# A four-layer graph network on one core: another order of the turns in the first stage, SAGE's weights multiplied while the lists are closed, and neighbour lists transposed by TensorE

## The chip, the cores and the metric

The kernel runs on one core of one Trainium2 chip. The metric is the time of one execution on the device in microseconds (us), lower is better; the given time is the median of three runs. Beside these there is one profiled execution, from which all durations of single instructions are taken.

A core has five engines that run their own queues in order and wait for each other through semaphores: TensorE (PE, matrix products), VectorE (DVE), ScalarE (ACT), GpSimd (POOL) and SyncE (SP). Here SyncE issues the ordinary transfers, GpSimd the gathers of single rows.

## The reference

Input are x (3327 x 512) and an adjacency matrix adj (3327 x 3327, 0 or 1). Four layers follow, each with a residual: `h = relu(layernorm(x)); x = x + layer(h, adj)`. Layers 0, 2 and 3 are graph attention with 8 heads of 64 columns, layer 1 is SAGE. Cut to what is computed:

```
# attention (layers 0, 2, 3), per head
Wh = h @ W
e  = leaky_relu(s_dst[i] + s_src[j], 0.2); e = where(adj > 0, e, -9e15)
out = softmax(e, over j) @ Wh        # layer 0: batch norm and relu; layers 2, 3: elu
# SAGE (layer 1)
agg = mask @ h / max(deg, 1)
out = relu(concat(h @ W_self + b_self, agg @ W_nb + b_nb) @ W_comb + b_comb)
```

In SAGE there is nothing between the two products, so W_self and W_nb can be multiplied by their halves of W_comb once, ahead of the data.

## The kernel before

The 3327 nodes are padded to 26 blocks of 128 rows (NB = 26). The adjacency is sparse and uneven, and the kernel lists for each of 52 groups of 64 rows which columns have any edge to the group. A fixed table, PLAN, says how many chunks of 128 columns a group takes whole ("dense") and how many chunks of listed columns. Attention then fetches rows of a table in DRAM, the dense ones by SyncE (line 1310), the listed ones by GpSimd's indirect gathers with the list idx as row numbers (line 1315).

The stages stand one after another:

1. **The turns** (`lists`, the loop over c at the end of the with block, and class `Projection`). Turn c handles three things. *Compare*: block c + 1 of adj is loaded as int32 (adj_i, line 1108, three buffers) and compared to 0 into a bf16 mask (adj_b, two buffers). Two blocks of three take a plain compare (line 1111) and are counted by ScalarE (`count`, line 1119); the third takes a compare with a sum (line 1113). `alone` (line 1122) sets one column from the count. *Words* (`gathered`): 26 small products of the mask with wsel pack 16 mask bits to a word (words_ps, line 1129); ScalarE copies the words out (line 1130), and VectorE derives from the same products which columns are absent from a group (none, line 1136). *Projection of layer 0* in a pipeline over turns: `first()` scales the products of block c - 3 into v_row (line 696), splits r_full into r_half and r_rest (lines 798 and 799), and transposes block c - 1 (h_ps, line 706); `second()` transposes r_half (tr_ps, line 724), and multiplies block c - 2 by the small and the large weight (sd_ps, line 739; wh_ps, line 742). SyncE writes table and r_dram (lines 699 and 729). After turns 3 and 6 `Products.layer` prepares small weights of other layers.
2. **Closing** (`closing`): VectorE adds up past (line 1145), TensorE makes 26 pairs of small products (shift_ps, lines 1149 and 1152), and then twelve passes over 3327 columns move each column number to its place in the list (lines 1164 to 1176); lines 1179 and 1180 leave the lists in shift, one group per partition: in partitions 0 to 63 the columns with exactly one edge to the group, in 64 to 127 those with several, which fill the group's chunks from the other end. Three last turns of the projection are interleaved with the first passes.
3. **Lists through DRAM**: SyncE and GpSimd write shift to DRAM (lines 1219, eight transfers each), read it back with one list chunk per row (line 1226), TensorE mirrors and adds the two halves by products with permutations (lines 1236 to 1241), and VectorE makes idx (lines 1246 to 1248). A fits test (lines 1251 to 1274) sets ok, on which a branch chooses the sparse path.
4. **Attention of layer 0** (`attend`): for each unit, VectorE makes the weights (mx, wgt, vw; lines 1544 to 1558) and TensorE accumulates facc (lines 1578 and 1589). Beside it runs a generator, `beside`: one step per unit, first SAGE's 8 weight products and 2 bias products of four 128x512 matrix products each (lines 1656 to 1681), then the sums for the batch norm (bsum_ps).
5. Batch norm, SAGE, and the attention of layers 2 and 3, which the change leaves alone.

In the stages 1, 2 and 4 the order on TensorE, VectorE and ScalarE is the order of the program, written out by hand (`manual_schedule`); SyncE's and GpSimd's queues, and all queues outside those blocks, are ordered by the compiler's scheduler. The loop that matters:

```
for c in range(NB):
    proj.first()
    alone(c)
    compare(c + 1)
    gathered(c)
    proj.second()
    count(c + 1)
```

## Time and profile before

| | |
|---|---|
| median of three runs | 2641.61 us (2631.7 to 2646.2) |
| profiled execution, its own time | 2360.66 us |
| its span | 2358.9 us |
| mean granted TensorE clock | 0.868 |
| TensorE busy | 1853.9 us (79%) |
| VectorE busy | 1703.4 us (72%) |
| ScalarE busy | 1102.6 us (47%) |
| GpSimd busy | 1167.0 us (49%) |
| DMA | 562.66 MB, mean 239 GB/s |

The page divides the span by engine, then by line; views of the trace give a stretch of time, the instructions in order of time, and the waits. In a row of the timeline stand the start (us), the duration (us), engine, line and operation, the tiles written and read, the shape, and in brackets how long the engine had been idle and what ended that. A row of stretches gives its length and then busy time and number of instructions for TensorE's products, its weight loads, VectorE, ScalarE and GpSimd, then the granted clock (1 is full), the DMA engines' share and GB/s. A row of waits gives the sum in us, how often, and the longest.

### The profile page before, as it was taken

Reading aid. Unit: us, or ns where it says so; the run is one execution under the profiler, and the core shown is the slowest. Engines: PE = TensorE matmul, PEld = TensorE weight load, DVE = VectorE, ACT = ScalarE, POOL = GpSimd, SP = SyncE. Lnnn points to the kernel's source line nnn. Section 1 sums busy time; section 2 is a strip of 40 time slices with the busy share of each in tenths; the row PEclk is TensorE's granted clock in tenths of the full one; section 3 lists DMA queues with packets and bytes.
Section 4 is the critical chain, followed back from the end, with each engine's and each line's share of the span. In section 5 each row is a group of like instructions: output and inputs, shape, how many; then the busy total and the mean of one; then the engine's idle time right before and its main releaser. Section 6 shows DMA issues by size and latency. Waiting matters only on the chain. (4 is left out here: it accounts for less than half of the span.)

```text
span 2358.9 us, 42783 instructions
## 1 busy us (share of the span) xinstructions
PE 1853.9 (79%) x14795; PEld 1033.1 (44%) x14795; DVE 1703.4 (72%) x3061; ACT 1102.6 (47%) x4123; POOL 1167.0 (49%) x1227
## 2 busy tenths in 40 slices
PE   5888316897888769899999947889888857777875
PEld 4555204454545424233333325555454435544443
DVE  5555966888889984044555559888777749999996
ACT  3566102355666644133333203678887812444543
POOL 1000023566777500477777536655655236776772
PEclk8788657999999979999999967889889867788787
DMA  7776118897889655688888698787777458888883
GB/s 278 261 286 234 32 68 294 272 326 261 266 257 296 216 187 205 217 252 258 265 257 264 207 280 273 238 254 241 226 242 240 137 209 251 272 281 261 278 284 116
DMA packets 205951, 562.66 MB, mean 239 GB/s; under 512 B 37359, under 2 KB 43597, under 8 KB 202399
## 3 DMA queue, kind: packets, MB, share of 16 engines
q0 software_dynamic: 93504, 328.25, 45.0%
q1 hardware_dynamic: 112222, 231.59, 28.3%
q8 instruction: 120, 1.97, 0.3%
q14 instruction: 105, 0.85, 0.1%
HBM read 496.47 MB, written 63.25 MB: 237 GB/s over the span
## 5 line engine op out<-in xcount | busy, mean ns | idle before, releaser
L1315 POOL DMA_INDIRECT rows_e<-table,idx x654 | 627.3, 959 | 358.2 <-issue 151.5
L1578 PE MATMUL facc<-vw,ones_of 128*64 128x260 f32 x2616 | 445.2, 455 | 73.6 <-DVE vw L1544 58.4
L1589 PE MATMUL facc<-rows_s,wgt 128*64 128x65 f32 x7200 | 349.1, 249 | 166.5 <-DVE wgt L1558 112.4
L1589 PEld LDWEIGHTS facc<-rows_s,wgt 128*64 128x64 f32 x7200 | 294.9, 159 | 286.6 <-DVE wgt L1558 140.6
L1544 DVE TENSOR_TENSOR vw<-rows_e,w_of 128x1040 f32<-128x1040 f32 (+1 forms) x270 | 395.7, 1466 | 9.5
L1315 POOL DMA_INDIRECT z_rows<-z_dram,idx x291 | 279.7, 961 | 228.9 <-PE sage_acc L1867 154.1
L1315 POOL DMA_INDIRECT rows_s<-table,idx x219 | 212.7, 971 | 228.9 <-PE facc L1589 147.4
L1558 DVE TENSOR_TENSOR wgt<-mx,mask 128x1024 f32<-128x1024 f32 (+1 forms) x255 | 280.3, 1099 | 42.4 <-ACT mask L1456 26.0
L1554 DVE TENSOR_TENSOR mx<-r_bc,rows_s 128x1024 f32<-128x1024 f32 (+1 forms) x255 | 280.6, 1101 | 40.5 <-DMA rows_s<-table 28.6
L1405 ACT ACTIVATE fhp<-sums,rd 64x64 f32<-64x64 f32 x816 | 215.6, 334 | 185.2 <-DVE rd L1398 177.3
L1578 PEld LDWEIGHTS facc<-vw,ones_of 128*64 128x64 f32 x2616 | 196.5, 156 | 219.9 <-issue 91.4
L1867 PE MATMUL sage_acc<-z_rows,z_mask 128*64 128x512 f32 x622 | 165.4, 604 | 13.0 <-DMA z_rows<-z_dram,idx 12.8
L1219 POOL DMA_DIRECT2D list_b<-shift x8 | 4.1, 515 | 316.5 <-DVE shift L1180 316.5
L1818 DVE TENSOR_TENSOR s_o<-n_ps,sage_b 128x512 f32<-128x512 f32 x26 | 18.0, 692 | 167.0 <-PE n_ps L1815 163.3
L1850 ACT CAST z_mask<-mask 128x128 f32<-128x128 uint8 (+1 forms) x201 | 51.3, 287 | 162.2 <-PE sage_acc L1867 159.9
L742 PE MATMUL wh_ps<-fWt,hT 128*128 128x512 f32 x208 | 121.3, 737 | 0.0
L1392 ACT COPY sums<-facc 128x260 f32<-128x260 f32 x153 | 56.3, 368 | 136.4 <-PE facc L1578 135.2
L1405 ACT ACTIVATE bn_y<-sums,rd 64x64 f32<-64x64 f32 x408 | 107.7, 334 | 2.9 <-DVE rd L1398 1.3
L1496 DVE TENSOR_REDUCE w_of<-r_of 128x16 f32<-128x48 f32 (+1 forms) x270 | 61.4, 227 | 62.1 <-PE r_of L1488 37.0
L1815 PE MATMUL n_ps<-fWx,bn_y 128*128 128x512 f32 x208 | 97.3, 610 | 0.0
L1352 PE MATMUL r_bc<-r_two,fones 2*128 2x512 f32 x156 | 85.3, 547 | 14.4 <-DMA r_two<-r_dram 8.8
L924 PE MATMUL p_wh<-fWt,hT 128*128 128x512 f32 x208 | 96.0, 605 | 0.3 <-ACT hT L919 0.3
(260 smaller groups left out, 2888.5 us busy)
## 6 DMA issues: line engine op xcount, KB each, us to landing
adj_i<-in_adj SPq DMA_DIRECT2D x26, 1664.0 KB
rows_s<-table SPq DMA_DIRECT2D x46, 528.0 KB
table<-v_row SPq DMA_DIRECT2D x78, 264.0 KB
rows_s<-table SPq DMA_DIRECT2D x62, 264.0 KB
rows_s<-table SPq DMA_DIRECT2D x23, 632.0 KB
fin_x<-fx SPq DMA_DIRECT2D x52, 256.0 KB
rows_e<-table,idx POOLq DMA_INDIRECT x654
rows_s<-table SPq DMA_DIRECT2D x31, 316.0 KB
```

The source lines that it names most:

```text
L742: nc.tensor.matmul(wh, hT[:, kc, :], self.Wt[:, kc, :], start=(kc == 0), stop=(kc == KC - 1))
L924: nc.tensor.matmul(wh, hT[:, kc, :], self.Wt[:, kc, :], start=(kc == 0), stop=(kc == KC - 1))
L1315: nc.gpsimd.indirect_dma_start(out=dst, out_offset=None, in_=src[:, :], in_offset=bass.IndirectOffsetOnAxis(ap=idx[:, k : k + 1], axis=0))
L1352: nc.tensor.matmul(rb, ones[0:2, :].bitcast(F32R), rrs.pop(j).bitcast(F32R), start=True, stop=True)
L1405: nc.scalar.mul(hp[o0 : o0 + GB, h * F : (h + 1) * F], sm[mine, q, 0:F], rd[mine, q, :])
L1544: nc.vector.tensor_tensor(vw[:, :n], gt[:, :n, : H * (F + 1)].rearrange("p k (h x) -> p k h x", x=F + 1), w[:, :n].unsqueeze(3).to_broadca ...
L1554: nc.vector.tensor_tensor(mx[:, :n], rbs[j].unsqueeze(1).to_broadcast(full), T.unsqueeze(3).to_broadcast(full), ALU.max)
L1558: nc.vector.tensor_tensor(wt[:, :n], mx[:, :n], mk.unsqueeze(2).to_broadcast(full), ALU.mult)
L1578: nc.tensor.matmul(accs[g][v * GB : (v + 1) * GB, :sw].rearrange("p (q x) -> p q x", x=F + 1), ones_of[i][:, k, :], by[:, v], start=f, stop=l,
L1589: nc.tensor.matmul(accs[g][v * GB : (v + 1) * GB, q * (F + 1) : (q + 1) * (F + 1)], wt[:, k, h, :], gt[:, k, h * (F + 1) : (h + 1) * (F + 1)],
L1815: nc.tensor.matmul(ps, y[:, b, kc * P : (kc + 1) * P], Wx[:, 0, kc, :], start=(kc == 0), stop=(kc == KC - 1))
L1867: nc.tensor.matmul(acc[u * GB : (u + 1) * GB, :], m, z, start=f, stop=l)
```

## The change

- *Turns*: `compare(c + 1)` moves to the head of the turn, and `second()` ahead of `gathered(c)`. The buffers stay three and two.
- *SAGE's weights*: the weight and bias products leave `beside` and become a generator `merged()`, stepped six times after each of the later passes of the closing and to its end behind them. They use the buffers of adj_i and the words' PSUM ring; their results still go to wx_dram, from where attention of layer 0 loads them (`w2`) as its generator's first act.
- *Fits*: the test becomes `fits()`, called between the sixth and the seventh pass of the closing; the counts' reciprocals go with it.
- *Lists*: no DRAM. TensorE transposes the 64 x 128 pieces of shift, mirrors the upper half by products with rev, and adds both in PSUM. A list's columns are now at k * 64 + g, so idx grows from 291 to 640 columns, and the gathers' column numbers follow.

```diff
-        self.first, self.n, self.at, self.nm = [], 0, [], 0
-        for g, (dense, mixed, pure) in enumerate(PLAN):
-            self.first.append(self.n)
-            self.n += mixed + pure
+        self.at, self.nm, self.most = [], 0, max(m + p for _, m, p in PLAN)
+        for dense, mixed, pure in PLAN:
             self.at.append(self.nm)
             self.nm += dense + mixed + pure
...
         dense, mixed, pure = PLAN[g]
-        f = self.first[g]
-        src = [(True, c) for c in range(dense)] + [(False, f + pure + k) for k in range(mixed)]
-        src += [(False, f + k) for k in range(pure)]
+        src = [(True, c) for c in range(dense)] + [(False, (pure + k) * HALF + g) for k in range(mixed)]
+        src += [(False, k * HALF + g) for k in range(pure)]
         return [(self.at[g] + i, d, k) for i, (d, k) in enumerate(src)]
...
+        capr = lp.tile([1, 2, G], F32, name="cap_row")
+        for g, (_, mixed, pure) in enumerate(PLAN):
+            for k, n in enumerate((mixed + pure, mixed)):
+                if g == 0 or PLAN[g][1:] != PLAN[g - 1][1:]:
+                    e = next((j for j in range(g, G) if PLAN[j][1:] != PLAN[g][1:]), G)
+                    nc.vector.memset(capr[:, k, g:e], float((2 - k) * NP - n * P))
+        nc.sync.dma_start(bias, t["L1_gnn_b_comb"].partition_broadcast(P))
...
+            def fits():
+
+                hp_ = lps.tile([1, 2, HALF], F32, name="none_ps", tag="words_ps")
+                nc.tensor.matmul(
+                    hp_.rearrange("p c g -> p (c g)"),
+                    ones_bf[:, 0:1],
+                    past[:, NB, :, :].rearrange("p c g -> p (c g)"),
+                    start=True,
+                    stop=True,
+                )
+                hr = lp.tile([1, 2, HALF], F32, name="none_row")
+                nc.vector.tensor_copy(hr, hp_)
+                nc.vector.tensor_tensor(hr[:, 0, :G], hr[:, 0, :G], hr[:, 1, :G], ALU.add)
+                nc.vector.tensor_tensor(capr, capr, hr[:, :, :G], ALU.subtract)
+                over = lp.tile([1, 1], F32, name="over")
+                nc.vector.tensor_reduce(over, capr.rearrange("p k g -> p (k g)"), AX.X, ALU.max)
+                fit = lp.tile([1, 1], I32, name="fit")
+                nc.vector.tensor_scalar(fit, over, 0.0, None, ALU.is_le)
+                nc.vector.tensor_tensor(prods.ok, prods.ok, fit, ALU.mult)
+                nc.vector.tensor_scalar_max(rdeg, rdeg, 1.0)
+                nc.vector.reciprocal(rdeg, rdeg)
+
+            def merged():
+
+                def held():
+                    w = ap.tile([P, NP], I32, name="adj_i", tag="adj_i", bufs=3)
+                    return w.bitcast(F32)
+
+                spot = held()[:, : 6 * D].rearrange("p (k o) -> p k o", o=D)
+                cols, Wcs = [], []
+                for k, bn in enumerate(("L1_bs", "L1_bn")):
+                    Wc = held()[:, : KC * D].rearrange("p (k o) -> p k o", o=D)
+                    nc.sync.dma_start(Wc, t["L1_gnn_W_comb"][k * D : (k + 1) * D, :].rearrange("(kc p) o -> p kc o", p=P))
+                    bcol = lp.tile([P, KC, 1], F32, name=f"b_col{k}")
+                    nc.sync.dma_start(bcol[:, :, 0], t[bn])
+                    cols.append(bcol)
+                    Wcs.append(Wc)
+                yield
+                ps = None
+                for k, wn in enumerate(("L1_WsT", "L1_WnT")):
+                    Wc = Wcs[k]
+                    for fc in range(KC):
+                        nc.sync.dma_start(spot[:, 2 + fc % 2, :], t[wn][fc, :, :, :].rearrange("p k o -> p (k o)"))
+                        if fc == 0:
+                            yield
+                            b_bc = spot[:, k, :].rearrange("p (k o) -> p k o", o=P)
+                            nc.scalar.copy(b_bc, cols[k].to_broadcast([P, KC, P]))
+                            ps = lps.tile([P, D], F32, name="fb_ps", tag="words_ps")
+                            for kc in range(KC):
+                                nc.tensor.matmul(ps, b_bc[:, kc, :], Wc[:, kc, :], start=(kc == 0), stop=(kc == KC - 1))
+                                yield
+                            nc.vector.tensor_tensor(bias, bias, ps, ALU.add)
+                        else:
+                            yield
+                        WT = spot[:, 2 + fc % 2, :].rearrange("p (k o) -> p k o", o=P)
+                        ps = lps.tile([P, D], F32, name="fwx_ps", tag="words_ps")
+                        for kc in range(KC):
+                            nc.tensor.matmul(ps, WT[:, kc, :], Wc[:, kc, :], start=(kc == 0), stop=(kc == KC - 1))
+                            yield
+                        nc.scalar.copy(spot[:, 4 + fc % 2, :], ps)
+                        nc.sync.dma_start(wx_dram[k, fc, :, :], spot[:, 4 + fc % 2, :])
+
             prods.layer(0, lps, "words_ps")
             compare(0)
             count(0)
             proj.begin()
             for c in range(NB):
+                compare(c + 1)
                 proj.first()
                 alone(c)
-                compare(c + 1)
+                proj.second()
                 gathered(c)
-                proj.second()
                 count(c + 1)
                 if c in (3, 6):
                     prods.layer(c // 3, lps, "words_ps")
@@ -1198,84 +1247,58 @@
                 table[:, ROW:].rearrange("(c p) w -> p c w", p=P),
                 words.rearrange("p c b w -> p c (b w)").bitcast(I32),
             )
-            close = closing()
+            close, make = closing(), merged()
             next(close)
+            next(make)
             while proj.left():
                 proj.first()
                 next(close, None)
                 proj.second()
                 next(close, None)
+            fits()
             for _ in close:
+                for _ in range(6):
+                    next(make, None)
+            for _ in make:
                 pass
 
...
-        zero = lp.tile([P, P], F32, name="zero")
-        nc.gpsimd.memset(zero, 0.0)
-        ra = lp.tile([P, NT, P], F32, name="rows_a")
-        rb = lp.tile([P, NT, P], F32, name="rows_b")
-        for i, (dst, p0, rows_) in enumerate(((la, 0, ra), (lb, HALF, rb))):
-            eng = (nc.sync, nc.gpsimd)[i]
-            for g0, ng, cap in ls.runs:
-                f = ls.first[g0]
-                eng.dma_start(
-                    dst[f : f + ng * cap, :].rearrange("(g k) e -> g (k e)", k=cap),
-                    shift[p0 + g0 : p0 + g0 + ng, : cap * P],
-                )
-            if NT * P > NCH:
-                eng.dma_start(dst[NCH:, :], zero[: NT * P - NCH, :])
-            for q in range(NT):
-                eng.dma_start(rows_[:, q, :], dst[q * P : (q + 1) * P, :])
         with tc.tile_pool(name="lset2_ps", bufs=1, space=PSUM) as lps:
-            slots = lp.tile([P, NT * P], F32, name="slots")
-            per = lp.tile([P, NT, NT * P], F32, name="perm")
-            for q in range(NT):
-                nc.vector.tensor_scalar(per[:, q, :], mir, float(q * P), None, ALU.is_equal)
-            tb = lp.tile([P, NT * P], F32, name="tb")
-            assert NT * P <= BANK
-            pa = lps.tile([P, BANK], F32, name="pa", tag="pa")
-            for q in range(NT):
-                nc.tensor.matmul(pa[:, : NT * P], rb[:, q, :], per[:, q, :], start=(q == 0), stop=(q == NT - 1))
-            nc.vector.tensor_copy(tb, pa[:, : NT * P])
-            pb = lps.tile([P, BANK], F32, name="pb", tag="pb")
-            nc.tensor.matmul(pb[:, : NT * P], rev, tb, start=True, stop=False)
-            for q in range(NT):
-                nc.tensor.matmul(pb[:, q * P : (q + 1) * P], ra[:, q, :], ident, start=False, stop=(q == NT - 1))
-            nc.vector.tensor_copy(slots, pb[:, : NT * P])
-
-            s = slots[:, :NCH]
-            nv = lp.tile([P, NCH], F32, name="nv")
-            nc.vector.tensor_scalar(nv, s, 0.0, float(NP), ALU.is_equal, ALU.mult)
-            nc.vector.tensor_tensor(nv, nv, s, ALU.add)
-            nc.vector.tensor_scalar(idx, nv, -1.0, float(NP - 1), ALU.add, ALU.min)
...
+            per = BANK // HALF
+            lo, hi = slice(0, HALF), slice(HALF, 2 * HALF)
+            tb = lp.tile([P, J, HALF], F32, name="tb")
+            for r0 in range(0, J, per):
+                n = min(per, J - r0)
+                pb = proj.psum.tile([P, per, HALF], F32, name="pb", tag="wh_ps", bufs=2)
+                for r in range(r0, r0 + n):
+                    j = J - 1 - r
+                    nc.tensor.matmul(
+                        pb[:, r - r0, :], shift[hi, j * P : (j + 1) * P], ident[hi, hi], start=(r == r0), stop=(r == r0 + n - 1)
+                    )
+                (nc.scalar.copy if r0 else nc.vector.tensor_copy)(tb[:, r0 : r0 + n, :], pb[:, :n, :])
+            s = lps.tile([P, -(-J // per) * per, HALF], F32, name="slots", tag="slots")
+            for r0 in range(0, J, per):
+                n = min(per, J - r0)
+                for k in range(r0, r0 + n):
+                    nc.tensor.matmul(s[:, k, :], shift[lo, k * P : (k + 1) * P], ident[lo, lo], start=(k == r0), stop=False)
+                last = [(g0, ng, cap) for g0, ng, cap in ls.runs if cap > r0]
+                for i, (g0, ng, cap) in enumerate(last):
+                    m = min(cap, r0 + n) - r0
+                    nc.tensor.matmul(
+                        s[:, r0 : r0 + m, g0 : g0 + ng],
+                        rev,
+                        tb[:, J - cap + r0 : J - cap + r0 + m, g0 : g0 + ng],
+                        start=False,
+                        stop=(i == len(last) - 1),
+                    )
+            nv = lp.tile([P, J, HALF], F32, name="nv")
+            nc.vector.tensor_scalar(nv, s[:, :J, :], 0.0, float(NP), ALU.is_equal, ALU.mult)
+            nc.vector.scalar_tensor_tensor(
+                idx.rearrange("p (k g) -> p k g", g=HALF), nv, -1.0, s[:, :J, :], ALU.add, ALU.add
             )
...
-            nc.sync.dma_start(bias, t["L1_gnn_b_comb"].partition_broadcast(P))
...
-                Wc = work[:, : KC * D].rearrange("p (k o) -> p k o", o=D)
-                nc.sync.dma_start(Wc, t["L1_gnn_W_comb"][k * D : (k + 1) * D, :].rearrange("(kc p) o -> p kc o", p=P))
-                bcol = wp.tile([P, KC, 1], F32, name="b_col", tag="b_col", bufs=1)
-                nc.sync.dma_start(bcol[:, :, 0], t[bn])
...
-                nc.vector.tensor_tensor(bias, bias, ps, ALU.add)
-                for fc in range(KC):
-                    WT = spot[1 + fc % 2].rearrange("p (k o) -> p k o", o=P)
-                    nc.sync.dma_start(WT, t[wn][fc, :, :, :])
-                    yield
-                    ps = wps.tile([P, D], F32, name="fwx_ps", tag="beside", bufs=1)
-                    for kc in range(KC):
-                        nc.tensor.matmul(ps, WT[:, kc, :], Wc[:, kc, :], start=(kc == 0), stop=(kc == KC - 1))
-                        yield
-                    nc.scalar.copy(spot[3], ps)
-                    nc.sync.dma_start(wx_dram[k, fc, :, :], spot[3])
...
-        idx = kp.tile([P, ls.n], I32, name="idx")
+        idx = kp.tile([P, ls.most * HALF], I32, name="idx")
         rdeg = kp.tile([P, NP // P], F32, name="rdeg")
+        bias = kp.tile([P, D], F32, name="sage_b")
+        wx_dram = ldram.tile([2, KC, P, D], F32, name="wx_dram")
```

## The prediction

> **What bounds the kernel now.** Outside the profiled span lie only 2360.66 - 2358.9 = 1.8 us, so sums are made in the span. The three timed runs have a median of 2641.6 us, 281 us more than the profiled execution; nothing in the profile says where these lie. I carry my difference over in microseconds; in proportion it would be 1.12 times as large.
>
> I read the busy shares of the page first, then the busy time by stretches: the change touches only the first 520 us.
>
> ```profile
> PE 1853.9 (79%) x14795; PEld 1033.1 (44%) x14795; DVE 1703.4 (72%) x3061; ACT 1102.6 (47%) x4123; POOL 1167.0 (49%) x1227
> ...
> 200.00:250.00 50.00, 46.46 (x311) 27.47 (x310) 32.64 (x93) 29.40 (x111) 0.00 (x0) 0.84 0.54 177
> 250.00:270.00 20.00, 6.63 (x16) 3.50 (x15) 17.35 (x19) 1.99 (x10) 0.00 (x0) 0.59 0.04 14
> 270.00:290.00 20.00, 4.40 (x8) 1.48 (x6) 19.69 (x16) 0.45 (x2) 0.00 (x0) 0.67 0.04 14
> 290.00:310.00 20.00, 0.00 (x0) 0.00 (x0) 19.55 (x14) 0.00 (x0) 0.00 (x0) 0.50 0.00 0
> ```
>
> No engine bounds the whole. Up to about 233 us the turns run (projection, compares, words); 245 to 325 us is VectorE alone, closing the lists, with TensorE and the DMAs (share 0.04) free; then the lists go through DRAM, and attention of layer 0 begins at 343 us. These stages are serial, so a microsecond in one is a microsecond of the end.
>
> Next, the waits inside the turns, and from the timeline a turn at full clock, the start of another, and one with a stall:
>
> ```profile
> DVE v_row L696 <- PE wh_ps L742: 30.0, 14, 4.8
> PE words_ps L1129 <- DVE adj_b L1122: 27.1, 15, 4.4
> DVE adj_b L1111 <- DMA adj_i<-in_adj: 19.6, 10, 3.8
> ```
>
> ```profile
> 226.60 0.27 PE L724 MATMUL tr_ps<-fident,r_half 128*16 128x128 f32 x1
> 227.52 3.68 PE L742 MATMUL wh_ps<-fWt,hT 128*128 128x512 f32 x8
> 231.03 0.60 PE L706 MATMUL h_ps<-fident,ln_x 128*128 128x128 f32 x4
> 231.47 0.91 PE L1129 MATMUL words_ps<-wsel,adj_b 128*128 128x10 bf16 x26
> ```
>
> ```profile
> 129.86 0.19 PE L1129 MATMUL words_ps<-wsel,adj_b 128*128 128x10 bf16 x1 [2.30 <-DVE adj_b L1122]
> 129.90 0.37 PE L724 MATMUL tr_ps<-fident,r_half 128*16 128x128 f32 x1
> 130.07 3.62 DVE L1113 TENSOR_SCALAR_CACHE_REDUCE adj_b<-adj_i 128x3328 bf16<-128x3328 int32 x1 [0.26 <-DMA adj_i<-in_adj]
> 131.64 5.79 PE L742 MATMUL wh_ps<-fWt,hT 128*128 128x512 f32 x8
> ...
> 138.29 1.88 DVE L1111 TENSOR_SCALAR adj_b<-adj_i 128x3328 bf16<-128x3328 int32 x1
> ```
>
> The reader is to see that a turn costs TensorE 5.6 us (226.60 to 232.24 between two transposes tr_ps) if nothing stalls, that the long compare (3.6 us) lies under the wh_ps products, and that after a stall of 2.30 us the same products take 5.79 instead of 3.68 us.
>
> **The turns.** In the changed program's queues VectorE's order becomes: none of block c, compare of c+2, v_row, r_half; TensorE's: h_ps, tr_ps, sd_ps, wh_ps, then words of block c. none waits for ScalarE's copy of the words, and tr_ps waits for r_half. So the end of one turn's words releases copy, none, compare, v_row, r_half, and only then the next tr_ps: the compare, hidden before, stands in TensorE's path. What waits behind it is v_row and r_half on VectorE, all products behind tr_ps on TensorE, and on SyncE the table's write.
>
> The gap, by starts in the trace: ScalarE's copy 0.35 (L1130) with 0.09 of hand-over; none 0.23 (140.09 to 140.32); compare 1.80 (138.29 to 140.09) or 3.54 (130.07 to 133.61); v_row 0.60 (137.47 to 138.07); r_half and hand-over 0.22. Sum 3.29, or 5.03 us in every third turn. The transposes h_ps (0.60) fall inside it. TensorE from tr_ps to the words' end: 0.92 + 3.51 + 0.91 = 5.34 us. So 8.63 or 10.37 us a turn at full clock.
>
> The clock: the stall of TensorE before the last words' product and the length of the wh_ps behind it, over the stage: 1.38, 1.99, 2.30, 2.57, 3.43 and 4.39 us gave 5.06, 5.98, 5.79, 5.36, 5.04 and 6.42 us; of six stalls under 1 us two gave over 5 us, four 3.68. From tr_ps to the end of wh_ps these six took 7.71, 7.53, 6.28, 6.29, 6.77 and 7.96, mean 7.09 against 4.60: 2.5 us lost. [...] By the rows, where 1.38 us was enough six times in six, all 22 turns lose 2.5 us: 55 us. I take the rows.
>
> From tr_ps of turn 3 to the last words' end, before: 39.76 to 232.38 = 192.6 us. After: turn 3 itself 5.34, 14 short turns of 8.63, 7 long of 10.37, turn 25 without compare 1.49 + 5.34: 205.6; the clock 55; the two weight layers (32 small matmuls, 7.0 us at L507, run in a gap that is there anyway) 4 each, between 0 and 10: 268.6. **+76 us** (at full clock +21). DMA waits (20 + 4 us) vanish: adjacency loads are issued in the middle of turn k-3 for the compare in k-1, some 1.4 turns or 15 us, and landed in 7 us (141.49 to 148.56). ScalarE's count (3.0 + 0.2 us) moves behind the words' copy, ends 3.6 us after the words, when VectorE comes to its reader; hidden, and beyond that it delays only words, 5 us later. Turns 0 to 2 end about 2.5 us later (each compare precedes the products, and the fourth block's is long); after the last turn wh_ps no longer stands before the lists' products (-1.8: VectorE's 1.0 us wait at L1157, 0.8 of order).
>
> **SAGE's weights.** Moved: 40 products of 128x512 f32 (0.86 us each warm, two at 0.43 as in wh_ps), ten ScalarE copies of 0.6 us, two bias adds of 0.69, and SyncE's loads and stores of 6.3 MB. In the closing VectorE alone is the path: it gains the two adds and the fits (eight operations, 1.74 us): **+3.1**. Free of charge otherwise if TensorE is done when shift is ready. Its transposes stand behind all forty products in its queue. The first 4 run by 285 us; 36 start when none_row is copied, near 290.4 us of the old time: 36 x 0.86 + 2 for a cold start, and a last group that waits for the second bias add (323.3 + 3.5): 327 us, against shift at 325.5 + 3.1 = 328.6. Covered by 1.6 us only; cold they end at 290.4 + 36 x 1.72 = 352, 24 us late.
>
> What attention of layer 0 loses of work:
>
> ```profile
> 367.69 0.62 ACT L1666 COPY fmake<-b_col 128x512 f32<-128x512 f32 x1 [11.31 <-DMA b_col<-in_L_bs]
> 368.55 1.22 DVE L1558 TENSOR_TENSOR wgt<-mx,mask 128x1024 f32<-128x1024 f32 x1 [7.03 <-ACT mask L1456]
> ```
>
> ScalarE stood at the copy of b_col, the mask behind it, VectorE 7.0 us for the mask. From 360 to 515 us (the last copy of the weights) VectorE was busy 123.6 us, 0.80; from 550 to 800 us 220.8 us, 0.88. At that rate 123.6 us take 140: -15. By bytes: 6.3 MB at the 290 GB/s of that stretch, -22. Against it, the 2 MB load of fWx moves from 519 us to the attention's first loads and lies ahead of rows on SyncE: up to 7 us. I take **-17**, between -7 (the stall alone) and -28.
>
> **The lists.** From shift's end to idx and the gathers:
>
> ```profile
> 324.00 1.49 DVE L1180 SCALAR_TENSOR_TENSOR shift<-at,shift 128x1280 f32<-128x1280 uint16 x1
> 325.52 2.47 SPq L1219 DMA_DIRECT2D list_a<-shift  x8
> 332.94 4.21 PE L1236 MATMUL pa<-perm,rows_b 128*128 128x384 f32 x6 [56.00 <-DMA rows_b<-list_b]
> 340.97 0.29 DVE L1248 TENSOR_SCALAR idx<-nv 128x291 int32<-128x291 f32 x1
> 343.82 1.04 POOL L1315 DMA_INDIRECT rows_e<-table,idx  x1 [11.27 <-SPq L1979]
> ```
>
> 325.5 to 341.3 = 15.7 us, with SyncE's and POOL's list transfers. Instead: ten 64-column products (128x65 f32, L1589: 16 in 1.15 to 2.00 us) 0.8 to the eighth, copy 0.69 (512 wide), eleven mirrored products 1.4, two operations on 640 columns 0.82 each (from 512 at 0.69), hand-overs 0.3: 4.9 us. **-10.8**, between -8 and -12.
>
> **Sum:** 2.5 + 76 - 1.8 + 3.1 - 17 - 10.8 = **+52 us**: 2413 profiled, 2641.6 + 52 = **2694 us**.
>
> **Rivals.** *The clock holds* (ends on the other side): [...] against it, six of six. Without the 55 us the sum is -3: 2639; with the 28 us end of the attention -14: 2628. It turns the sign when a turn loses under 0.14 us (3 over 22), and leaves no measurable change up to 0.7. 2612 to 2655. *TensorE bounds the closing*: the page's clock there is 0.5 to 0.67; if forty products stay cold, transposes start 24 us late: 2718. Against it: products without a pause ran at 3.68 in a row. *The transfers come back*: in the timed runs' extra 281 us loads may be slower and the old turns wait longer for adj_i (23 us here); were they doubled, the change would save 23 us more: 2671. *The change does not do what it says*: compares one block ahead cannot run ahead at all, as none stands before them; that is in the forecast.
>
> **How the numbers follow.** Forecast 0.54 (own range 2655 to 2730), clock holds 0.26, closing 0.11, slower loads 0.09 (2640 to 2690). Range 2622 to 2732: it leaves out some 0.11 of the clock case and 0.07 above. About 0.5% (13 us) is what a measurement can tell: faster (under 2628) has half of the clock case and 0.02 of the forecast's tail, 0.15; same has the other half and a third of the slower loads, 0.16; slower 0.69.
>
> **What would show it.** Right: turns of 11 to 13 us, tr_ps waiting for r_half in all of them, no wait for adj_i, wh_ps over 5 us; last words near 310 us; shift to idx in 5 us; attention 0 some 17 us shorter. Wrong: wh_ps at 3.68 us in most turns (the clock), TensorE still in weights when shift is ready (closing), or attention as long as before.

## The result, and the profile after

The changed kernel takes 2682.79 us (median of 4 runs, 2681.03 to 2685.33) against 2640.78 us for the kernel before on the same chip (4 runs, 2631.7 to 2646.2): ratio 1.0163, 95% interval 1.0133 to 1.0194, so 42 us slower. 2694 us was predicted, +52.

The profiled execution of the changed kernel has a span of 2682.4 us at a mean granted clock of 0.825. It can't be set beside the first profile of the kernel before, which was 281 us shorter than that kernel's timed runs; a second profile of it, run e1 below, took 2618.6 us. The two by landmarks of the trace (starts; "shift ready" is the end of the last operation on shift; the last ScalarE operation on bn_mean closes attention of layer 0):

| stretch | before (e1) | after | difference | predicted |
|---|---|---|---|---|
| start to last copy of words | 236.9 | 312.0 | +75.1 | +78.5 |
| to shift ready | 92.1 | 93.5 | +1.4 | +1.3 |
| to the first gather by idx | 17.9 | 12.7 | -5.2 | -10.8 |
| to the end of attention 0 | 572.0 | 552.4 | -19.6 | -17 |
| to the end | 1697.7 | 1711.7 | +14.0 | 0 |

The first four rows make +51.7 us. The last is not touched by the change; over the traces of one level of speed shown below it lies anywhere from 1692 to 1731 us, so the two profiles alone would say +66 where the medians say +42. The first row rests on the copies of the words (first and last start at the end of the times), in e1 and in the changed kernel:

```profile
L1130 ACT CAST words<-words_ps x26: 332/344/352, 21.9 to 236.9; 128x208 uint16<-128x208 f32 x26
```

```profile
L1117 ACT CAST words<-words_ps x26: 312/332/344, 27.5 to 312.0; 128x208 uint16<-128x208 f32 x26
```

This landmark moves from trace to trace even where the turns are the same: it is 231.3, 233.2, 236.9 and 240.7 us in the four traces with the old order (e3, the first profile, e1, e6), and 285.4 and 293.2 in e9 and e10. Of a difference of less than some 10 us in it between single traces nothing can be said.

The waits between 10 and 312 us of the changed kernel (waiting engine, tile and line, what it waited for: sum in us, times, longest):

```profile
DVE none L1123 <- ACT words L1117: 110.3, 24, 6.4
ACT words L1117 <- PE words_ps L1116: 98.2, 23, 5.4
...
PE tr_ps L721 <- DVE adj_b L1109: 40.2, 11, 4.8
...
PE tr_ps L721 <- ACT adj_s L1106: 20.0, 7, 2.9
```

Before, in the first profile, three waits of VectorE and TensorE shared some 77 us here, for wh_ps, the mask and adj_i. Now VectorE stands at none for the words' copy 24 times, 110 us, and 18 waits of TensorE at tr_ps make 60 us. The names behind these last two rows are only those of semaphores that came last by the record; what tr_ps reads is r_half, as the timeline of one turn shows:

```profile
182.69 0.27 PE L721 MATMUL tr_ps<-fident,r_half 128*16 128x128 f32 x1 [2.86 <-ACT adj_s L1106]
183.61 5.38 PE L739 MATMUL wh_ps<-fWt,hT 128*128 128x512 f32 x8
188.82 0.80 PE L1116 MATMUL words_ps<-wsel,adj_b 128*128 128x10 bf16 x26
...
189.65 0.33 ACT L1117 CAST words<-words_ps 128x208 uint16<-128x208 f32 x1 [3.13 <-PE words_ps L1116]
190.02 0.33 DVE L1123 TENSOR_SCALAR none<-words_ps 128x50 bf16<-128x50 f32 x2 [4.07 <-ACT words L1117]
190.26 3.61 DVE L1100 TENSOR_SCALAR_CACHE_REDUCE adj_b<-adj_i 128x3328 bf16<-128x3328 int32 x1
193.79 0.69 DVE L693 TENSOR_TENSOR v_row<-wh_ps,v_row 128x512 f32<-128x512 f32 x1
194.40 0.16 DVE L795 TENSOR_TENSOR r_half<-r_full,r_half 128x8 fp32r<-128x8 f32 x1
...
194.70 0.37 PE L721 MATMUL tr_ps<-fident,r_half 128*16 128x128 f32 x1 [4.59 <-DVE r_rest L796]
```

Words, their copy, none, the long compare of 3.61 us, v_row, r_half, and only then the next transpose: the chain of the forecast, link by link, in a turn of 12.0 us. The products wh_ps take 5.38 us and not 3.68, after a gap of 2.86 us.

The end of the closing and the lists:

```profile
404.05 1.49 DVE L1167 SCALAR_TENSOR_TENSOR shift<-at,shift 128x1280 f32<-128x1280 uint16 x1
404.74 0.59 PE L1226 MATMUL fwx_ps<-adj_i 128*128 128x512 f32 x1
405.60 2.11 PE L1274 MATMUL pb<-fident,shift 64*128 64x64 f32 x17 [0.26 <-DVE shift L1167]
...
409.45 3.66 PE L1286 MATMUL slots<-tb,rev 128*128 128x8 f32 x16
413.04 1.11 PE L1282 MATMUL slots<-fident,shift 64*128 64x64 f32 x4
414.09 1.44 PE L1286 MATMUL slots<-tb,rev 128*128 128x1 f32 x6
415.63 0.82 DVE L1294 TENSOR_SCALAR nv<-slots 128x640 f32<-128x640 f32 x1 [7.31 <-PE slots L1286]
```

The last weight product ends at 405.33 us, shift at 405.54: the cover of the weights was 0.2 us, forecast at 1.6. From there to idx (417.31 us) pass 11.8 us, where 4.9 were forecast: 3.85 us of transposes, 6.1 us of mirrored products, from 409.45 on at 0.23 us an instruction, and 1.7 us of VectorE's two operations.

### The profile page after: what moved, and what is told of

Same layout as the page of the kernel before. It is cut to its first block, busy times and chain, and to the rows that moved or that the text cites. A ratio compares the mean times of both kernels' runs of the same rounds, so it can differ in the third digit from the quotient of the medians.

```text
span 2682.4 us, 42828 instructions
## 1 busy us (share of the span) xinstructions
PE 2014.5 (75%) x14843; PEld 1123.2 (42%) x14843; DVE 1703.8 (64%) x3056; ACT 1103.7 (41%) x4124; POOL 1155.2 (43%) x1205
## 5 line engine op out<-in xcount | busy, mean ns | idle before, releaser
L1601 PE MATMUL facc<-vw,ones_of 128*64 128x260 f32 x2616 | 496.2, 485 | 98.7 <-DVE vw L1567 58.5
L1612 PE MATMUL facc<-rows_s,wgt 128*64 128x65 f32 x7200 | 398.0, 257 | 223.9 <-issue 133.4
L1612 PEld LDWEIGHTS facc<-rows_s,wgt 128*64 128x64 f32 x7200 | 330.5, 165 | 344.7 <-issue 214.0
L1577 DVE TENSOR_TENSOR mx<-r_bc,rows_s 128x1024 f32<-128x1024 f32 (+1 forms) x255 | 280.4, 1100 | 63.6 <-DMA rows_s<-table 17.9
L1601 PEld LDWEIGHTS facc<-vw,ones_of 128*64 128x64 f32 x2616 | 211.9, 166 | 249.7 <-issue 158.0
L921 PE MATMUL p_wh<-fWt,hT 128*128 128x512 f32 x208 | 109.8, 677 | 52.7 <-ACT hT L916 27.5
L739 PE MATMUL wh_ps<-fWt,hT 128*128 128x512 f32 x208 | 144.5, 860 | 0.0
L978 PE MATMUL p_wh<-fWt,hT 128*128 128x512 f32 x184 | 97.3, 678 | 1.7 <-issue 1.7
```

What stands on the lines that cost most here:

```text
L739: nc.tensor.matmul(wh, hT[:, kc, :], self.Wt[:, kc, :], start=(kc == 0), stop=(kc == KC - 1))
L921: nc.tensor.matmul(wh, hT[:, kc, :], self.Wt[:, kc, :], start=(kc == 0), stop=(kc == KC - 1))
L978: nc.tensor.matmul(wh, hT[:, kc, :], self.Wt[:, kc, :], start=(kc == 0), stop=(kc == KC - 1))
L1577: nc.vector.tensor_tensor(mx[:, :n], rbs[j].unsqueeze(1).to_broadcast(full), T.unsqueeze(3).to_broadcast(full), ALU.max)
L1601: nc.tensor.matmul(accs[g][v * GB : (v + 1) * GB, :sw].rearrange("p (q x) -> p q x", x=F + 1), ones_of[i][:, k, :], by[:, v], start=f, stop=l,
L1612: nc.tensor.matmul(accs[g][v * GB : (v + 1) * GB, q * (F + 1) : (q + 1) * (F + 1)], wt[:, k, h, :], gt[:, k, h * (F + 1) : (h + 1) * (F + 1)],
```

## The experiments

The theory was: (1) none stands ahead of the compare in VectorE's queue and waits for the words, so the compare lies in TensorE's path; (2) the gap that this makes lowers TensorE's clock; (3) the moved weights and the lists pay, each on its own. The rivals: the mask buffers or the loads and not none; nothing of the clock; the 281 us as a cause of their own; TensorE late in the closing.

**e1: the kernel before, profiled again**, with no edit.

> The kernel before once more, unchanged, for a trace taken beside those of the variants. Theory (the turns cost it, the rest is the same): last words near 232 us as in the first trace, first gather near 344 us, and whatever the whole takes more than 2361 us lies behind that, spread over the gathers, as it does in the changed kernel's trace (2264 us from the first gather to the end against 2015). Rival (the first trace's turns were lucky): last words 20 us or more later than 232, so that the change cost less in the turns than the two traces say.

It took 2618.6 us; the landmarks are in the table above. Attention 0, one row of stretches for the first and one for the second profile of the same program, each 572 us from its first gather:

```profile
343.00:915.00 572.00, 452.39 (x4346) 268.65 (x4347) 476.72 (x839) 300.69 (x945) 310.83 (x317) 0.92 0.81 267
```

```profile
347.00:919.00 572.00, 433.82 (x4162) 259.69 (x4162) 399.48 (x671) 258.79 (x858) 310.61 (x317) 0.87 0.74 232
```

The last number is GB/s: 267 against 232. VectorE finished 839 instructions in the one and 671 in the other. Attention 0 lasted 488.6 us in the first profile (343.8 to 832.4) and 572.0 here, while the last copy of the words moved only from 233.2 to 236.9 us and the first gather from 343.8 to 347.0. So of the 258 us by which the two traces differ all but 3 lie behind the first gather, where rows are fetched, and the turns can be compared across both profiles. The rival that slower loads lengthen the old turns is out; the waits for adj_i in them are 25.5 us here and 23.4 in the first profile:

```profile
DVE adj_b L1111 <- DMA adj_i<-in_adj: 20.2, 12, 3.7
...
DVE adj_b L1113 <- DMA adj_i<-in_adj: 5.3, 3, 2.0
```

**e2: the turns alone**, the kernel before with the new order of the loop.

```diff
+                compare(c + 1)
                 proj.first()
                 alone(c)
-                compare(c + 1)
-                gathered(c)
                 proj.second()
+                gathered(c)
```

> The kernel before with the new order of the turns alone; weights and lists as before. Theory: turns of 10.3 and 12.0 us as in the changed kernel, last words near 312 us, and the whole near 2640 + 79 = 2719 us. Rival (the turns are hidden by loads in the timed runs, and the loss lies in the moved weights and the wider lists): within 20 us of 2640.

2703.55 us (2684.71 to 2710.4), ratio 1.0248 (1.0174 to 1.0321), so some 65 to 72 us slower than the kernel before (79 was expected; the four runs spread over 26 us); the last copy of the words starts at 309.8 us, 72.9 later than in e1. Attention 0 is 571.6 us long, as before. The turns alone lose more than the whole change does.

**e3: everything but the turns**, the changed kernel with the old order of the loop (the same edit, reversed).

> The changed kernel with the old order of the turns; weights and lists as changed. Theory: 2683 - 79 = 2604 us, that is 36 us under the kernel before: the two other parts gain some 30 to 40 us. Rival: 2640 to 2683, the two other parts gain nothing or cost.

2607.51 us, ratio 0.9904 (0.988 to 0.9929): faster than both kernels. The last copy of the words at 231.3, the first gather at 338.3 (8.7 earlier than in e1), attention 0 553.4 us long (18.6 shorter). So the other parts gain about 24 us, and the loss of the change is all in its turns.

**e4: the clock**. From turn 3 on, three or five unread products of 128x512 a turn (warm, into a bank of their own) stand between h_ps and tr_ps and fill TensorE's gap; the rest of the computation is complete.

```diff
+            spare = lps.tile([P, D], F32, name="warm_ps", tag="warm_ps", bufs=1)
...
                 alone(c)
+                if c >= 3:
+                    warm(3 if summed(c + 1) else 5)
                 proj.second()
```

> The changed kernel with three (before a long compare's turn five) idle products of 128x512 between h_ps and tr_ps of each turn, read by nobody, so that TensorE's gap is filled and nothing else moves. Theory (the clock drops in the gap): wh_ps at 3.7 instead of 5.4 us, turns of 8.6 and 10.4 us, 22 turns x 1.7 us = 37 us less than the changed kernel: 2645 us. Rival (the turn's serial chain alone costs it, the clock is as slow for another reason): wh_ps stays at 5.4 us and the time within 8 us of 2683.

The last copy of the words starts at 273.6 us instead of 312.0, and the kernel takes 2653.79 us (2645 was expected), ratio 1.0111 (1.0079 to 1.0142). The wh_ps instructions, two to a product, of the changed kernel and of e4 (minimum/median/maximum ns), with the row of e4's words' copies:

```profile
L739 PE MATMUL wh_ps<-fWt,hT x208: 592/906/1201, 33.2 to 351.7; 128*128 128x512 f32 x104
```

```profile
L739 PE MATMUL wh_ps<-fWt,hT x208: 592/592/1201, 33.1 to 312.3; 128*128 128x512 f32 x104
...
L1117 ACT CAST words<-words_ps x26: 310/333/344, 27.4 to 273.6; 128x208 uint16<-128x208 f32 x26
```

The turns of e4 are 8.6 us, and 10.3 with the long compare: the forecast's 8.63 and 10.37 at full clock. The changed kernel's run 10.3 to 12.0. Work was added and the stage became 38.4 us shorter, so the clock is a cause of its own, worth 38 of the 75 us in this trace; with it gone the order of the turns still costs 36.7 us. Its size is less sure than that it acts: the execution traced took 2622.01 us and was the fastest of 13, the medians of the changed kernel and of e4 lie 29 us apart, and their ratios to the kernel before differ by 0.005, some 14 us.

**e5: none a turn later, and a third mask buffer.** The two operations on none leave gathered and become absent, which turn c does for block c - 1, behind v_row and r_half.

```diff
-                    m = masks[c] = ap.tile([P, NP], BF16, name="adj_b", tag="adj_b", bufs=2)
+                    m = masks[c] = ap.tile([P, NP], BF16, name="adj_b", tag="adj_b", bufs=3)
...
                 compare(c + 1)
                 proj.first()
+                absent(c - 1)
                 alone(c)
```

> The changed program with one thing undone in its turns: none of block c is made in turn c+1, behind v_row and r_half, and there is a third mask buffer, so that no instruction that waits for the words of block c stands before the compare in VectorE's queue. Theory (none, queued before the compare, puts it into TensorE's path): the compare runs under the products again, turns of 6 to 8 us instead of 10.3 and 12, wh_ps at 3.7 us in most of them, last words at 200 to 236 us instead of 312, the time 2583 to 2608 us (2683 less 75 to 100). Rival (the compare stays in the path because its block's load or the words themselves are late, or the clock stays low whatever the order): last words at 290 us or later, 2660 us or more.

2618.74 us, ratio 0.9948 (0.9926 to 0.9969), last copy of the words at 243.9 us. 68 of the 75 us are gone, so what e5 undoes, none ahead of the compare and the lack of a mask buffer, was the cause; e7 and e8 take the two apart. The gain was less than expected: the last words were to come by 236 us and the time to be 2608 or less. One turn of e5, below the row of its words' copies, shows what may be left:

```profile
L1117 ACT CAST words<-words_ps x26: 309/332/345, 27.5 to 243.9; 128x208 uint16<-128x208 f32 x26
...
172.35 2.98 ACT L1106 ACTIVATE adj_s<-adj_b 128x3328 bf16<-128x3328 bf16 x1
...
177.34 0.24 ACT L744 ACTIVATE v_row<-sd_ps,fdown 128x8 f32<-128x8 f32 x1
...
177.62 0.17 DVE L747 TENSOR_SCALAR s_col<-sd_ps 128x8 f32<-128x8 f32 x1 [1.91 <-ACT v_row L744]
...
178.52 3.59 DVE L1100 TENSOR_SCALAR_CACHE_REDUCE adj_b<-adj_i 128x3328 bf16<-128x3328 int32 x1
...
182.84 0.38 PE L721 MATMUL tr_ps<-fident,r_half 128*16 128x128 f32 x1 [4.36 <-DVE r_half L795]
```

ScalarE's count of 3 us stands ahead of its exponentials in v_row; VectorE's s_col waits for these, the compare stands behind s_col, and starts only at the words' end. Turns of 5.9 us alternate with 10.1 and 8.5. This is read from the rows; no run moves the count alone.

**e7 and e8: each half of e5 alone.** e7 has none a turn later and two masks, e8 three masks and none where the change has it. Each was executed once.

> As the run with none a turn later, but with the two mask buffers that the changed program has. Theory: the compare of block c+2 then waits for the words of block c by its buffer, so it still starts only when they end; the gap loses only ScalarE's copy and none (0.7 us a turn): turns 9.6 and 11.3 us, last words near 297 us, 2668 us. Rival (only none's place matters): last words at 200 to 236 us as with three masks.

> The changed program with a third mask buffer and nothing else. Theory: none of block c still stands before the compare of c+2 in VectorE's queue, so nothing moves: turns 10.3 and 12 us, last words at 310 to 314 us, 2683 us within 12. Rival (the mask buffer is what makes the compare wait): turns of 6 to 8 us, last words under 240 us, 2610 us or less.

e7: 2671.06 us, last copy at 293.8, most turns of 9.6 to 11.3 us. The wait has a new name:

```profile
DVE adj_b L1098 <- PE words_ps L1116: 63.3, 13, 5.8
...
DVE adj_b L1100 <- PE words_ps L1116: 23.0, 8, 5.2
```

e8: 2681.43 us, turns of 10.3 and 12.0 as in the changed kernel; its last words came at 320.7 us, some 9 us later than in the changed kernel; between 39 and 120 us the granted clock was 0.67 in it, 0.78 in the changed kernel. Two things hold the compare at the words' end, none ahead of it in the queue and the mask buffer that the words still read. Either alone suffices: taking away the mask's hold alone buys nothing, taking none out of the way alone 18 us, of the 68 that both buy together.

**e6: the lists alone** (and the fits in the closing): the changed kernel with the old turns and SAGE's weights back beside attention 0.

```diff
-            close, make = closing(), merged()
+            close = closing()
-            next(make)
...
-                for _ in range(6):
-                    next(make, None)
-            for _ in make:
```

> Of the change only the lists by TensorE transposes (and the fits in the closing) are kept; the turns have their old order, and SAGE's weights are made beside attention of layer 0 as before. Theory (lists 5 to 6 us, the weights' move 17 to 20 us in attention): last words near 233 us, first gather near 341, attention 572 us long as in the kernel before, the time some 6 us under the kernel before and 18 us over the old-turns kernel: 2626 us. Rival (the 20 us that attention lost come from the lists' different placing of idx, or from DRAM traffic of the lists, and not from the weights): attention near 552, time near 2608.

2631.94 us, ratio 1.001 (0.9984 to 1.0035): the 6 us that were expected do not show, though the interval leaves room for 4. Attention 0 is 567.7 us long, 14.3 more than with the weights moved (e3), so the weights shorten it. The lists, shift to first gather, took 15.9 us, where e1 took 17.9 and e3 12.2:

```profile
334.64 3.86 PE L1270 MATMUL pb<-fident,shift 64*128 64x64 f32 x17 [50.16 <-DVE shift L1167]
...
341.69 3.66 PE L1282 MATMUL slots<-tb,rev 128*128 128x8 f32 x16
...
334.60:346.00 11.40, 11.36 (x56) 11.17 (x56) 0.69 (x1) 0.27 (x1) 0.00 (x0) 0.50 0.00 0
```

TensorE had been idle for 50 us, and 17 transposes took 3.86 us; behind the weight products they took 2.11. The last row is the stretch of all these products: busy for 11.36 of 11.40 us, TensorE stayed at a granted clock of 0.50. So the weights in the closing serve the lists too: parts that were added up on their own in the forecast are not independent.

**e9 and e10.** e9 tries to remove what e5 left: compares two blocks ahead, and the count before the words' copy.

```diff
+            compare(1)
             for c in range(NB):
-                compare(c + 1)
+                compare(c + 2)
...
                 proj.second()
-                gathered(c)
                 count(c + 1)
+                gathered(c)
```

> The run with none a turn later and three masks, with two more moves: compares stand two blocks ahead, and ScalarE's count of the next block stands before its copy of the words instead of after it, so that it no longer delays the copies of hT and the exponentials of the next turn, which VectorE's s_col and the compare behind it waited for. Theory (what was left of the exposed compare came from ScalarE's count): no turn waits for the compare, turns of 5.6 to 7 us, wh_ps at 3.7 us, last words at 195 to 215 us, the time 2571 to 2595 us. Rival (adjacency loads then set the turn, or the clock stays low): last words at 230 us or later, 2607 us or more.

It did not: 2665.98 us, ratio 1.0132 (1.0089 to 1.0174), last copy at 285.4 us. Its waits between 10 and 290 us:

```profile
PE tr_ps L721 <- DVE r_half L795: 53.6, 19, 3.9
...
DVE adj_b L1098 <- PE words_ps L1116: 47.0, 11, 5.8
...
DVE adj_b L1100 <- PE words_ps L1116: 26.5, 7, 4.9
```

With three masks, the compare of block c + 2 needs the buffer of block c - 1, whose words end just before v_row of turn c, behind that compare: e7's chain, one block on. I had counted buffers and not asked when the last reader of each is done.

e10, executed once, is e9 with eight unread products of 128x512 among the lists' small ones.

> The same with unread products of 128x512 put among the lists' transposes and mirrored products, which add 0.85 us each, about 7 of them. Theory (the lists' 62 small instructions take 0.23 us instead of 0.12 because the clock was halved while they ran): the small ones take 0.12 to 0.14 us throughout, and shift to idx stays within 11 to 13.5 us in spite of 6 us of added products. Rival (they take 0.23 us for their weight loads, whatever the clock): shift to idx 17 to 18 us.

Stretches with the small products, of the changed kernel and of e10 (TensorE busy first, the granted clock third from the end):

```profile
409.40:415.50 6.10, 6.10 (x27) 5.76 (x26) 0.00 (x0) 0.00 (x0) 0.00 (x0) 0.50 0.63 227
```

```profile
391.00:397.00 6.00, 6.00 (x34) 4.16 (x33) 0.00 (x0) 0.00 (x0) 0.00 (x0) 1.00 0.71 256
```

In the changed kernel TensorE was busy for all of 6.10 us and ran at half clock. With large products between, the clock is 1.00, and 16 transposes take 2.00 us. Shift to idx was 16.9 us, more than expected and close to the rival's 17 to 18, so the sum does not decide between the two; the duration of the small products does. By the starts of what follows them the eight added ones cost 1.06 us each twice and 0.89 to 0.97 the other six times, 7.8 us in all, which leaves 9.1 us for the lists at full clock (62 instructions at 0.12, and 1.7 us of VectorE). So of the 6.9 us that were missing against the forecast (11.8 less 4.9) some 3 are the clock and 4 the number of instructions.

**e11: e9 with a fourth mask buffer**, one number in the program.

> The two-ahead run with a fourth mask buffer and nothing else. In the two-ahead run the compare of block c+2 still waited for the words of block c-1 by its buffer (73 us of such waits), and those words end just before v_row of turn c, which stands behind that compare: the same chain one block on. Theory (a compare that stands n blocks ahead needs n+2 mask buffers before it leaves TensorE's path): no compare waits for words, turns of 5.6 to 7.5 us, last words at 200 to 230 us instead of 285, the time 2585 to 2612 us. Rival (loads of adjacency, which the fast turns then ask for at 1.7 MB in 6 us, or ScalarE, set the turn at 8 us or more): last words at 240 us or later, 2618 us or more.

2323.23 us against 2359.74 us for the kernel before in the same runs: ratio 0.9836 (0.9808 to 0.9863), the lowest of all versions. In this set of runs the kernel before itself was at the level of its first profile, so e11's trace (span 2320.6) is read beside that one (2358.9): last copy of the words at 224.0 against 233.2, first gather at 329.7 against 343.8 (14.1 us earlier), attention 0 464.3 us against 488.6 (24.3 shorter), together 38.4 us. Its waits between 10 and 225 us:

```profile
PE tr_ps L721 <- DVE r_half L795: 24.3, 13, 5.0
...
DVE adj_b L1098 <- DMA adj_i<-in_adj: 15.5, 6, 6.2
...
DVE adj_b L1100 <- DMA adj_i<-in_adj: 13.0, 6, 3.8
```

No compare waits for words any more. Most turns take 5.6 to 10.9 us, and what delays the compare in the long ones is its load, 28.5 us. For these the rival of that run holds, though the last words came within the range of its theory. The turns end only 9 us earlier than before, no more than this landmark moves by itself; the gain lies mostly in attention 0.

## Why the prediction was right, and where not

*The turns* (+78.5 forecast, +75.1 measured): right in the chain and in the sum, but not in the two parts of the sum. At full clock +23.5 was forecast (2.5 ahead of turn 3, 21 behind it), and e4 has +36.7; for the clock 55 was forecast, and e4 won back 38. The errors cancel, so the closeness of the sum is in part luck. Regular turns at full clock were forecast at 8.63 and 10.37 us, and e4 has 8.6 and 10.3. The difference lies in the turns 3, 6 and 9, which hold the small weight products: 33.9 us forecast for the three (8.63 each and 4 for each weight layer, the third at nothing), 48.6 in e4 and 45.9 in the changed kernel. The waits for adj_i fell from 25.5 us in e1 to 5.3; they were to vanish. That the compares can't run ahead was named and is so; e5, e7 and e8 add that even without none the two masks would have held them.

*The clock*: forecast at 2.5 us in each of 22 turns, from six rows. In the 19 turns without small weight products the changed kernel takes 216.1 us and e4 174.7, 2.2 us a turn; in the other three e4 took 2.7 us more than the changed kernel, so that what the clock costs there stays open. In the turn shown TensorE stands idle for 2.86 us, but from the end of wh_ps to its next start, with only small products between, pass 4.9 us: from 178.71 (173.33 + 5.38, the wh_ps of the turn before) to 183.61. Counted in this second way the rows of both kernels separate. Of 15 such gaps of up to 3.10 us, 14 were followed by wh_ps of 3.68 us (the other, of 2.81 us, by 5.38); all 35 gaps of 3.68 us and more were followed by 5.04 us or more. In the traces of both kernels and of e1, e3, e5, e7, e8, e9 and e11, none with filled turns, no gap under 2.8 us made wh_ps longer and every gap over 4.5 us did; in between both occur. That small products in a gap do not keep the clock up was measured in the lists only, with products with the identity and those of few columns: a granted clock of 0.50 with TensorE busy for 6.10 of 6.10 us in the changed kernel, 1.00 in e10 with large products put between. For the turns it is my reading of the rows. It was not tested on its own, since e4 closed the gap altogether.

*SAGE's weights* (-17 forecast; e3 against e6 -14.3, after against e1 -19.6): right. The closing was covered, by 0.2 us where 1.6 was forecast, so nearly not.

*The lists* (-10.8 forecast, -5.2 measured to the first gather): this step failed. "Eleven mirrored products 1.4" took 6.1 us with the two transposes between them, and "ten 64-column products ... 0.8 to the eighth" took 3.85 us to the last that stands ahead of the mirrored ones. Two terms were mis-sized. An f32 product here is two instructions with a weight load each (20 of either for the ten transposes), 0.12 us apart at full clock (16 in 2.00 in e10), so 0.24 us a product; the forecast's 0.10 to 0.13 us a product is what the row that it went by, 16 in 1.15 to 2.00, gives for one instruction. And the lower half's transposes, which stand ahead of the mirrored products, were put at nothing: from the end of the copies of tb (408.34) to the first mirrored product they took 1.1 us more. Then the clock halves within the stage, some 3 us: it was 0.98 from 405.5 to 409.4 us and 0.50 from there to 415.5. The last 1.6 us before the gather came shorter than I had counted (idx to gather 2.6 us in e1, 1.0 after), which hides part of it.

*The rivals*: "the clock holds" is out by e4 and by the wh_ps of the changed kernel (a median of 906 ns an instruction, 592 in e4). "TensorE bounds the closing" did not come about, by 0.2 us. "The transfers come back" is out by e1. The sum of +52 holds in the trace to its end of attention 0 (+51.7), partly because the turns' 3.4 us and the attention's 2.6 us of error weigh against the lists' 5.6. Why the medians show 42 is not settled; the stages behind attention 0 differ by up to 39 us from one trace to the next.

## What to carry to other kernels

Before a step is moved ahead, list for each engine what stands in front of it in the queue *and* when the last reader of its output buffer is done: with one block of look-ahead more, a compare needs one buffer more (three at one block in e5, four at two in e11), and either obstacle alone voids the move. Look for the idle time of TensorE between large products, not between any products: in the lists of the changed kernel transposes and products of few columns kept TensorE busy for 6.10 of 6.10 us at a granted clock of 0.50, and with large products between them (e10) it was 1.00. And do not add up parts that share an engine's clock: the lists became 2.0 us shorter alone (e6 against e1) and 5.7 us behind the weight products (e3 against e1).

## What the hardware showed that was not expected

The clock fell to half while TensorE was 100% busy with small products: in the changed kernel the granted clock was 0.50 from 409.4 us, 4 us after the end of the last product of 512 columns (405.33), to 415.5 us. In e6, where TensorE had been idle for 50 us ahead of them, the same small products ran at 0.50 throughout, for 11.4 us.

The same program ran at two levels, 271 to 281 us apart: 2360.66 us in the first profile and 2359.74 in the median of 9 runs beside e11, 2631.75 to 2640.78 in the medians beside all other runs, at least once each on the same chip. In the two traces all but 3 us of it lies behind the first gather, at 267 against 232 GB/s in attention 0; the turns before it take 233.2 and 236.9 us. What sets the level was not found. Within each set of timed runs here all lay at one level, so the ratios hold; a profile can lie at the other, as the first one did, and times of different sets do not compare when their levels differ.
